# A graph layer with a fast convolution: tensor work moved off GpSimd, a first group that starts with its first weights, one pool of PSUM banks, and an instruction order from a model of three engines

## The chip, the cores and the metric

The kernel runs on one core of one Trainium2 chip, in fp32. The metric is the device time of one execution in microseconds (us). Each version was executed several times; nearly all times lie within 0.3% of their version's median. The engines are TensorE (PE in the profile; PEld is its weight load, which overlaps it), VectorE (DVE), ScalarE (ACT), GpSimd (POOL) and SyncE (SP, which issues most transfers). The profile shows one execution: for the kernel before a further one (2689 us, 0.6% under the median). So a span differs a little from the median.

## The reference

32 graphs of 512 nodes with 256 features go through a layer norm and a relu, then one graph layer, then a residual addition. Cut to what matters:

```python
h = jnp.maximum(_layernorm(x, axis=-1), 0.0)
# the graph layer, with x now meaning h and xc its transpose per graph
y  = relu(bn1(conv1d(xc, conv1_w, pad=0)))          # 1 tap, 256 -> 256
y  = bn2(conv1d(y, conv2_w, pad=8))                 # 17 taps, 256 -> 256
x_conv = relu(y + xc)
s = x @ w_se.T + b_se                               # 3 numbers for each node
dist = sq[:, :, None] + sq[:, None, :] - 2.0 * einsum('bnd,bmd->bnm', s, s)
A = exp(-dist) * mask                               # 512 x 512 for each graph
x_nmp = einsum('bnm,bmd->bnd', A, relu(x @ w_msg.T + b_msg))
gi, gh = concat([x_conv, x_nmp]) @ w_ih.T + b_ih, x @ w_hh.T + b_hh
r, z = sigmoid(gi_r + gh_r), sigmoid(gi_z + gh_z)
n = tanh(gi_n + r * gh_n)
out = x_before_the_norm + (1.0 - z) * n + z * x
```

## The kernel before

The 17-tap convolution is not done tap by tap. Four graphs form a group, there are 8 groups, and each group's convolution is a set of 25 small products (5 outer times 5 inner points of evaluation), so 200 products in all. A product needs a weight tile `w` of three 256x256 matrices (two taps and their sum) and an operand `x2` made from the first convolution's output. It multiplies the common column of `x2` by the sum `w[:, 2]` into PSUM tile `ps_b`, and the two differences `xd` by the two taps into `ps_c`: 12 matmuls where direct evaluation takes 16. VectorE adds the parts and puts the 25 products together again. Only then can a group's gates run, because they need all of its convolution.

The weights are made once on VectorE, ScalarE and GpSimd, written to DRAM, and read back for every group. No product may start before all 25 are made and a second lane of three graphs is through:

```python
    def ends(x2):
        xd = cv.tile([P, 2, RV], F32, name="xd", bufs=2)
        ...
        nc.gpsimd.tensor_tensor(
            xd, d02, x2[:, 1:2, :].to_broadcast([P, 2, RV]), op=ALU.subtract
        )
        return xd
    ...
            # in weights_first, for each of the 25 points
                w = cv.tile([P, 3, ND, D], F32, name="w", bufs=2)
                for i in range(ND):
                    nc.scalar.activation(
                        w[:, :2, i, :], next(inner[i]), AF.Copy, scale=GSCALE[j1] * GSCALE[j2]
                    )
                    yield
                nc.gpsimd.tensor_tensor(w[:, 2], w[:, 0], w[:, 1], op=ALU.add)
                if made is not None:
                    nc.scalar.dma_start(WD[made_w], made)
                    made_w += 1
    ...
    def convolution():
        wg = (w for _ in range(NG) for w in weights_again())
        yield lambda: made_w == 25 and not lanes[1].batches
        ...
                while len(WS) < min(m + 1 + AHEAD_W, 25 * NG):     # AHEAD_W is 1
                    WS.append(next(wg))
```

PSUM has eight banks here: two for `ps_c`, one for `ps_b`, two for the gates' `ps_acc`, two for `ps_g`, and one, `ps_tr`, that nearly all transposes by TensorE share:

```python
    gps = ctx.enter_context(tc.tile_pool(name="gps", bufs=2, space=PSUM))
    tr = ctx.enter_context(tc.tile_pool(name="tr", bufs=1, space=PSUM))
```

GpSimd also does the last three steps of the gates, and VectorE does the scaling of the layer norm:

```python
                nc.gpsimd.tensor_tensor(t, hT[:, o, :], r, op=ALU.subtract)
                nc.gpsimd.tensor_tensor(t, z, t, op=ALU.mult)
                nc.gpsimd.tensor_tensor(t, r, t, op=ALU.add)
```

The order of the instructions on each engine is fixed when the program is built. Streams of work (normalisation, graphs, convolution, gates, output) are Python generators; each reports how much PE time it has used, and a function `pace` hands out VectorE and ScalarE work in proportion to it, whether or not those engines are then free.

## Time and profile before

| | before |
|---|---|
| median of 3 runs (a fourth came with the comparison) | 2703.95 us (2698.34 to 2708.66) |
| span in the profile | 2687.0 us |
| PE work if every matmul ran back to back at full clock ("warm"; the prediction derives it) | 2074 us |
| end of product 25 (first group) | 419 us |
| mean granted PE clock | 0.925 |
| GpSimd tensor work that the change moves | 605 us |

The last row is the sum of the busy times of five kinds of GpSimd instruction: 283.2 (`xd`), 98.5, 94.8 and 93.1 (the gates' mixes) and 35.3 (the third weight matrix).

The way to read this kernel is as a ledger of PE. The span is PE's warm work plus what is lost, and what is lost is either idle PE or PE that is busy below its full clock. I keep this ledger for two stages, the start (until product 25 ends) and the rest. The ends of products are read from the records that write `ps_c`; the warm work that the program issues up to product 25 is counted from the instructions in their order. The prediction shows the lines.

### The profile page before, as it was taken

To read this page: it belongs to the slowest core of one execution; us is meant where nothing else is said; L and a number is where in the kernel's file an instruction comes from. 1 tells how busy PE (TensorE), PEld (TensorE's weight loads), DVE (VectorE), ACT (ScalarE), POOL (GpSimd) and SP (SyncE) were. 2 spreads that over 40 slices of the span, in tenths; PEclk is the share of its full clock that TensorE was granted. 3 is DMA by queue.
4 is the path that set the end of the run, shared out by engine and by line. 5 is a ranking of instruction groups with operands and counts; after the bars stand their busy time and mean duration, and the time that the engine had idled before them with its cause. 6 is when DMAs were issued, how large, how long until landed. Compare 5 with 4: busy or idle time off the path is not lost. (4 is left out here: it accounts for less than half of the span.)

```text
span 2687.0 us, 25967 instructions
## 1 busy us (share of the span) xinstructions
PE 2267.2 (84%) x9312; PEld 1385.3 (52%) x9312; DVE 1471.7 (55%) x2461; ACT 712.1 (27%) x1184; POOL 642.0 (24%) x468
## 2 busy tenths in 40 slices
PE   5537786888878899989899888998998899899998
PEld 2214665455445555555555555565555555555443
DVE  5663786455447556455646546575645555656311
ACT  3232223322324222332232421333231312211211
POOL 1130221121112212222212222222213222333222
PEclk8767898988989999989999999999999999999999
DMA  6464655344335434343444334554433333423211
GB/s 198 140 222 123 207 185 168 83 130 145 113 110 143 125 121 129 141 153 110 134 128 125 117 123 149 153 157 118 126 118 135 119 118 129 145 94 124 85 60 35
DMA packets 388240, 351.84 MB, mean 131 GB/s; under 512 B 280720, under 2 KB 330256, under 8 KB 387472
## 3 DMA queue, kind: packets, MB, share of 16 engines
q1 hardware_dynamic: 370688, 296.96, 36.9%
q10 hardware_dynamic: 17424, 53.22, 5.1%
q8 instruction: 74, 1.21, 0.2%
q14 instruction: 54, 0.44, 0.1%
HBM read 280.12 MB, written 69.99 MB: 130 GB/s over the span
## 5 line engine op out<-in xcount | busy, mean ns | idle before, releaser
L98 PEld LDWEIGHTS ps_c<-xd,w 128*128 128x128 f32 x3200 | 412.5, 205 | 88.7 <-issue 46.5
L98 PE MATMUL ps_c<-xd,w 128*128 128x116 f32 x3200 | 422.4, 289 | 35.8 <-POOL xd L345 35.8
L345 POOL TENSOR_TENSOR xd<-x 128x480 f32<-128x480 f32 x200 | 283.2, 1423 | 686.7 <-PE ps_c L98 296.2
L744 PE MATMUL ps_acc<-xconv,wih 128*128 128x512 f32 x768 | 372.8, 609 | 6.4 <-ACT xconv L755 6.4
L744 PE MATMUL ps_acc<-hTb,whh 128*128 128x512 f32 x768 | 371.7, 616 | 3.7 <-ACT r L763 3.7
L98 PE MATMUL ps_b<-x,w 128*128 128x116 f32 x1600 | 238.6, 297 | 152.0 <-DMA w<-wd 97.5
L744 PE MATMUL ps_acc<-xnb,wih 128*128 128x512 f32 x768 | 363.6, 596 | 0.0
L781 POOL TENSOR_TENSOR o_sb<-hTb,r 128x512 f32<-128x512 f32 x64 | 93.1, 1454 | 1014.8 <-ACT r L776 1014.8
L98 PEld LDWEIGHTS ps_b<-x,w 128*128 128x128 f32 x1600 | 223.6, 210 | 215.2 <-issue 151.9
L775 DVE TENSOR_TENSOR r<-ps_acc,r 128x512 f32<-128x512 f32 x64 | 44.2, 691 | 383.2 <-PE ps_acc L744 383.2
L646 PE MATMUL ps_g<-at,msg 128*128 128x512 f32 x464 | 220.7, 624 | 17.7 <-DVE at L640 17.5
L744 PEld LDWEIGHTS ps_acc<-hTb,whh 128*128 128x128 f32 x768 | 145.3, 198 | 158.7 <-issue 150.2
L744 PEld LDWEIGHTS ps_acc<-xconv,wih 128*128 128x128 f32 x768 | 142.5, 195 | 153.3 <-issue 141.5
L744 PEld LDWEIGHTS ps_acc<-xnb,wih 128*128 128x128 f32 x768 | 141.4, 191 | 153.8 <-issue 153.3
L567 ACT ACTIVATE mid<-ps_b 128x232 f32<-128x232 f32 x200 | 72.7, 363 | 423.4 <-PE ps_b L98 396.7
L304 DVE SCALAR_TENSOR_TENSOR x<-x,x 128x480 f32<-128x480 f32 (+1 forms) x184 | 169.4, 920 | 2.3
L766 DVE SCALAR_TENSOR_TENSOR r<-ps_acc,vec,r 128x512 f32<-128x512 f32 x64 | 48.0, 749 | 218.1 <-PE ps_acc L744 180.7
L646 PEld LDWEIGHTS ps_g<-at,msg 128*128 128x128 f32 x464 | 91.3, 202 | 132.5 <-issue 113.8
L592 DVE TENSOR_TENSOR msg<-ps_g,bmsg 128x256 f32<-128x256 f32 x116 | 48.8, 421 | 175.8 <-PE ps_g L98 175.7
L98 PE MATMUL ps_g<-wmsg,hT 128*128 128x259 f32 x464 | 124.3, 410 | 16.7 <-DVE aug L593 10.8
L295 DVE TENSOR_TENSOR x<-x 128x240 f32<-128x240 f32 (+1 forms) x200 | 132.5, 662 | 0.9
L443 DVE TENSOR_TENSOR n<-ps_c,mid 128x464 f32<-128x464 f32 x120 | 76.0, 633 | 88.6 <-PE ps_c L98 87.4
(119 smaller groups left out, 2690.4 us busy)
## 6 DMA issues: line engine op xcount, KB each, us to landing
w<-wd SPq DMA_DIRECT2D x200, 768.0 KB, 4.6
m_sb<-in_adj_dram SPq DMA_DIRECT2D x512, 64.0 KB, 2.5
wd<-w ACTq DMA_DIRECT2D x25, 768.0 KB, 3.5
hd<-hT ACTq DMA_DIRECT2D x32, 512.0 KB, 6.5
nd<-right ACTq DMA_DIRECT2D x64, 256.0 KB, 2.0
hTb<-hd SPq DMA_DIRECT2D x32, 512.0 KB, 5.1
xnb<-nd SPq DMA_DIRECT2D x64, 256.0 KB, 2.9
res<-in_x_dram SPq DMA_DIRECT2D x64, 256.0 KB, 5.0
```

Of the source, the lines that this page charges most:

```text
L98: nc.tensor.matmul(ps, lhsT, rhs, start=(i == 0), stop=(i == len(pairs) - 1))
L295: nc.vector.tensor_tensor(dst[:, :some, :], get(a, some), get(b, some), op=ALU.subtract)
L304: nc.vector.scalar_tensor_tensor(dst, a, -2.0, b, op0=ALU.mult, op1=ALU.add)
L345: nc.gpsimd.tensor_tensor(xd, d02, x2[:, 1:2, :].to_broadcast([P, 2, RV]), op=ALU.subtract)
L443: nc.vector.tensor_tensor(dst.rearrange("p (h n) -> p h n", h=2), ps.rearrange("p (h n) -> p h n", h=2), mid[:, None, :].to_broadcast([P, ...
L567: nc.scalar.activation(mid, ps, AF.Copy)
L592: nc.vector.tensor_tensor(msg[:, c, :], ps[:, :D], bmsg[:, :D], op=ALU.add)
L646: nc.tensor.matmul(ps, msg[:, c, d * P : (d + 1) * P], at[:, c, :], start=(c == 0), stop=(c == NT - 1))
L744: nc.tensor.matmul(ps, w[:, at + i, cols(o, g)], hT[:, i, :] if k == 0 else x_in[2 * k - 2 + i], start=(k == of[0] and i == 0), stop=(k == ...
L766: nc.vector.scalar_tensor_tensor(r, ps_h, vec[:, _COL["b_hh"] + 2 * ND + o : _COL["b_hh"] + 2 * ND + o + 1], r, op0=ALU.add, op1=ALU.mult,)
L775: nc.vector.tensor_tensor(r, ps_n, r, op=ALU.add)
L781: nc.gpsimd.tensor_tensor(t, hT[:, o, :], r, op=ALU.subtract)
```

## The change

The intent: use GpSimd for nothing but tiny square roots and a few transfers, so that it cannot hold up VectorE; let the first group begin as soon as its first weight exists; give transposes the same banks as other work; and let a model of the engines choose the order. The core of the diff, with cuts and with comments added here:

```diff
-    gps = ctx.enter_context(tc.tile_pool(name="gps", bufs=2, space=PSUM))
-    tr = ctx.enter_context(tc.tile_pool(name="tr", bufs=1, space=PSUM))
+    gps = ctx.enter_context(tc.tile_pool(name="gps", bufs=3, space=PSUM))
+    now = 10.0
+    class Engine:
+        def __getattr__(self, name):
+            def issue(*tiles, **more):
+                size = max(elements(t) for t in tiles if hasattr(t, "shape"))
+                self.free = max(self.free, now) + self.fixed + self.each * size
+                getattr(self.engine, name)(*tiles, **more)
+            return issue
+    dve, act = Engine(nc.vector, 0.12, 0.00108), Engine(nc.scalar, 0.16, 0.0009)
+    def matmul(ps, lhsT, rhs, **more):
+        nonlocal now
+        now += max(0.22, elements(ps) / 600.0)
+        nc.tensor.matmul(ps, lhsT, rhs, **more)
...
-        nc.gpsimd.tensor_tensor(                   # xd; the gates' three mixes alike
+        dve.tensor_tensor(
             xd, d02, x2[:, 1:2, :].to_broadcast([P, 2, RV]), op=ALU.subtract
         )
...
-            nc.vector.tensor_scalar(               # scaling of the layer norm
-                xs[:, c, :], xs[:, c, :], mv[:, c, 0:1], rstd[:, c : c + 1],
-                op0=ALU.subtract, op1=ALU.mult,
+            act.activation(
+                xs[:, c, :], xs[:, c, :], AF.Identity, bias=shift[:, c : c + 1],
+                scale=rstd[:, c : c + 1],
             )
...
-        yield lambda: made_w == 25 and not lanes[1].batches
+                yield lambda: len(X2) > m and len(WS) > m
+                yield max(X_AT[m], W_AT[m])
+                if g == 0:                         # no xd, no third weight
+                    d0, d1, d2 = sides(x2[:, 0, :]), sides(x2[:, 1, :]), sides(x2[:, 0, :], 1)
+                    product(ps[:, :NH], (0, d0), (1, d1))
+                    product(ps[:, NH:], (0, d1), (1, d2))
...
-    AHEAD, AHEAD_W = 3, 1                          # two weight buffers, one product ahead
+        return cv.tile([P, 3, ND, D], F32, name="w", bufs=3)
+                while 25 <= len(WS) < min(m + 3, 25 * NG):
+                    weights_again(len(WS))
...
+        if b < TURNED:                             # the first 8 graphs' masks: turned by PE
+            m, ps = gr.masks.pop((b, c)), bank()
+            for k in range(NT):
+                turn(ps[:, k * P : (k + 1) * P], m[:, k * P : (k + 1) * P])
...
-        credit = min(credit + pe * rate, 1.0)      # pace()
+        while dve.free < now + 0.5 and background():   # fill()
+            pass
```

The second lane of graphs goes too. Third weights are made on VectorE during the second group and sent to DRAM from there on.

## The prediction

> **What bounds the kernel now.** I read the page's busy shares and slices first, then the busy times of two stretches, then what TensorE (PE) waited for in the second of them, and last the durations of VectorE (DVE) instructions beside GpSimd (POOL) ones.
>
> ```profile
> PE 2267.2 (84%) x9312; PEld 1385.3 (52%) x9312; DVE 1471.7 (55%) x2461; ACT 712.1 (27%) x1184; POOL 642.0 (24%) x468
> ...
> PE   5537786888878899989899888998998899899998
> ...
> PEclk8767898988989999989999999999999999999999
> ```
>
> PE is the busy engine, and no other is over 55%. But slices 1 to 5 (some 67 us each) are poor in PE work, and in the same slices the granted clock is down to 0.6 to 0.8. So there are two stages: a start, and a long rest.
>
> How much PE time is needed? The chain of waits shows dense runs at full clock (start us, us, what):
>
> ```profile
> 2137.45 1.79 PE ps_c L98 x16
> ...
> 2546.00 25.77 PE ps_acc L744 x60
> ```
>
> An fp32 matmul is two records here, so a convolution matmul of 116 columns costs 2 x 0.111 us and a matmul of 512 columns 2 x 0.429 us. From the records' starts in dense runs, one of 259 columns costs 2 x 0.218 and a 128x128 transpose 0.109; the eight records of one exponential's four products take about 1.2 us together. Over the whole program: 4800 x 0.111 + (2304 + 512 + 256) x 0.429 + 512 x 0.218 + 672 x 0.109 + 32 x 1.2 = 2074 us. This "warm floor" is 77% of the 2687 us span; 613 us are lost to idleness and to the low clock.
>
> The first convolution product starts at 258 us, and the first group's 25th ends at 419 us (from the starts of the records that write ps_c). By then 204 us of warm work are done. The two stretches (columns: busy of PE, PE weight load, DVE, ACT, POOL, then the clock):
>
> ```profile
> 0.00:419.00 419.00, 263.18 (x1121) 173.28 (x1122) 257.67 (x524) 118.95 (x233) 87.59 (x80) 0.81 0.58 179
> 419.00:2687.00 2268.00, 2004.07 (x8193) 1212.03 (x8192) 1214.08 (x1937) 593.16 (x952) 554.39 (x388) 0.95 0.39 122
> ```
>
> Start: 419 - 204 = 215 us lost. Rest: 2074 - 204 = 1870 us of warm work in 2268, so 398 us lost: 264 us of idle PE (2268 - 2004) and 134 us in which PE was busy but slower than warm. What the idle PE of the rest waited for (us in total, times, longest):
>
> ```profile
> PE ps_b L98 <- DMA w<-wd: 75.5, 26, 7.9
> PE ps_c L98 <- POOL xd L345: 35.6, 17, 6.7
> PE ps_tr L659 <- DVE res L663: 31.6, 32, 3.4
> PE ps_tr L616 <- ACT left L613: 22.3, 23, 2.8
> PE ps_b L98 <- ACT at L634: 20.4, 8, 6.6
> PE ps_tr L260 <- ACT hT L261: 16.4, 15, 2.0
> ```
>
> These are not one bottleneck but many short waits: a weight tile with one product's warning, the POOL difference, and transposes that share one PSUM bank (ps_tr, 31.6 + 22.3 + 16.4 = 70 us).
>
> Last, what POOL does to DVE. First two groups of DVE instructions (min/median/max ns):
>
> ```profile
> L304 DVE SCALAR_TENSOR_TENSOR x<-x,x x184: 624/657/2699, 91.0 to 2480.5; 128x480 f32<-128x480 f32 x160, 128x1440 f32<-128x1440 f32 x24
> ...
> L775 DVE TENSOR_TENSOR r<-ps_acc,r x64: 681/692/693, 516.1 to 2674.8; 128x512 f32<-128x512 f32 x64
> ```
>
> Then one moment of the timelines of DVE and POOL (start us, us):
>
> ```profile
> 1362.13 1.72 DVE L295 TENSOR_TENSOR x<-x 128x480 f32<-128x480 f32 x1
> ...
> 1361.79 1.54 POOL L783 TENSOR_TENSOR o_sb<-r,o_sb 128x512 f32<-128x512 f32 x1
> ```
>
> L295 takes 0.65 us when POOL is quiet; here it sits out L783 and takes 1.72. L775, with one input in PSUM, never varies. Taking every DVE form at its median beside no POOL work instead of its mean, DVE's summed durations fall from 1596 to 1417 us: POOL costs DVE 178 us.
>
> **What the Trainium skill says.** "SBUF — State Buffer", Who interferes with whom: DVE and GpSimd share a port pair under an exclusive lock; a DVE instruction with two SBUF inputs contends with GpSimd instructions that read SBUF, one with at most one SBUF input outside the two-port modes does not. The trace agrees, by L304 against L775 and by the single-input SBUF scaling L239 (406 ns, up to 1355). "GPSIMD Engine Reference", 4.1 Engine selection: two-input elementwise work is about twice as slow there as on DVE. Agrees: xd, 480 elements, is 1.20 us at the median on POOL, and DVE's undisturbed two-input form of that size 0.65. "TensorE: Matmul & The Clock Gate", HAM oscillation: idle gaps put the PE clock back to half. Agrees: the clock records hold only 0.5 and 1.0, and the poor slices are the cold ones.
>
> **The change, part by part.**
>
> *Work on PE.* The first group's products use both taps directly: 16 matmuls for 12, so 25 x 4 x 0.222 = +22 us. Eight graphs' masks are transposed on PE: 128 x 0.109 = +14. New floor 2110 us.
>
> *Start.* Before, 25 products waited for all 25 weights, written to DRAM and read back, and for three graphs of a second lane. Now each product goes once its own weight exists. In the new PE order the four first conv1 pairs (in the old kernel done at 72 us, with 12 us of waiting behind exponentials and a batch's transposes) come before any exponential, and the raw weights (issued at 31 us behind 19 mask loads) are asked for ahead of the masks. I choose 48 us for the first product: the fourth normalisation ended at 30 us before, and transposes, conv1 and six us of first operands follow. The new order shows 204 us of warm PE work up to product 25, of which some 17 lie before the first product. DVE must in the same time make weights (10 of 1.75 us and 50 of 0.69 = 52), operands of a group (47), the group's sums (34), six graphs (6 x 6) and six normalisations' statistics (15): 184 us. Neither engine has slack over the other, so I choose 85% of PE's warm rate: 48 + 187 / 0.85 = 268, say 270 us for product 25, against 419. That is the largest term, about -150.
>
> *DVE.* Gains 175 xd x 0.65 = 114, 192 gate mixes x 0.68 = 131, 25 third weights x 0.69 = 17, 32 small shifts 5: +267. Loses 128 scalings x 0.405 = 52 (to ACT), 32 mask transposes x 0.72 = 23, 25 first-group sums x 0.63 = 16 (to ACT): -91. Loses the lock: -178. Net -2: everything POOL did fits into the time POOL cost DVE. Over a shorter span DVE rises to about 61%.
>
> *ACT.* 128 scalings x 0.56 (the like-sized h with scale and bias) = +72, the first group's copies +14, its mids -9; its order has 52 table switches for 46 at 1.28 us, +8. About 800 us, no bound.
>
> *Rest.* Warm work 2110 - 204 = 1906. Idle: weights now come two products ahead in three buffers (I take 60 of 75), xd is ready on DVE a product ahead (30 of 36), transposes rotate through three banks with everything else (55 of 76, the 70 plus 5.5 us of L659 waiting on POOL): -145. Cold time shrinks in proportion, 134 x 145 / 264 = -74. Against this I set +45 of new waits, because DVE is in order and now holds xd and the mixes too. Lost: 398 - 145 - 74 + 45 = 224. Rest: 1906 + 224 = 2130.
>
> Sum: 270 + 2130 = 2400 us.
>
> **The rivals.** (1) *The new order brings as many waits as it removes.* It is fixed at build time from estimated durations; where they are off, an in-order engine holds everything behind it. A row load is no longer asked for one batch ahead, and four rows stand between two groups' operands. For it: PE idle is already spread over many small causes. Against: the named ones are structural and really go. The rest then keeps its 1870 / 2268 = 0.825: 1906 / 0.825 + 270 = 2580. (2) *DVE becomes the bound.* For it: more two-input work, and the start needs 184 us of it. Against: 61% on average. If the start runs at DVE's pace with gaps, product 25 falls at 320 and the rest loses 40 more: 2490. (3) *The order works as meant*, and PE runs the rest at 0.93, as the old kernel's last gates do (31.9 warm us in each 34.3 us round): 1906 / 0.93 + 260 = 2310. (4) *The start is hidden anyway.* Against it: no gate can run before the first group ends, so its 150 us cannot be won back elsewhere. A slower kernel would need 290 us of new waits over my sum; I see no source of that size.
>
> **Range and chances.** Rival 3 sets the low end, 2310; rival 2 with 20 us to spare sets the high end, 2510, so that rival 1 in full lies outside. The 2% line is 2650, above even rival 1: faster 0.95, same 0.04, slower 0.01.
>
> **What would show it.** First product near 48 us and product 25 near 270; POOL busy under 60 us; L304's maximum near its median for its form; DVE busy within 60 us of 1472; PE's waits for w and for the transposes' bank mostly gone; mean clock 0.97 or more. Wrong if product 25 comes after 320, if the rest runs under 0.85 of warm, or if PE waits long for DVE's xd or mixes.

## The result, and the profile after

| | before | after |
|---|---|---|
| median | 2702.93 us (4 runs) | 2331.05 us (4 runs, 2323.61 to 2335.55) |
| span in the profile | 2687.0 us | 2331.6 us |
| first product starts | 258 us | 54 us |
| product 25 ends | 419 us | 287 us |
| DVE: excess over undisturbed durations | 178 us | 1 us |

The ratio of the two is 0.8621 (95% interval 0.8591 to 0.865). Ratios are computed as the mean time of one kernel's runs over that of the other's of the same rounds, so they are not quite the ratio of the medians quoted.

The page of the kernel after: busy shares, PE and its clock in 40 slices, and the chain of work that ended last by engine:

```profile
PE 2186.6 (94%) x9640; PEld 1359.6 (58%) x9640; DVE 1453.7 (62%) x2700; ACT 783.0 (34%) x1318; POOL 60.6 (3%) x73
...
PE   5888989999989999999989998999999999999998
...
PEclk9998989999999999999999999999999999999999
...
PE 83%; DVE 6%; ACT 5%; DMA 4%; issue 1%; SPq 0%; ACTq 0%; DVEq 0%
```

One poor slice is left at the start, where five were; the clock is 0.975 on average; and 83% of the chain is PE's own work. GpSimd is down to 60.6 us. The kernel is now bound by PE in the plain sense.

The busy times of the two stretches, start and rest, in the columns that the prediction names:

```profile
0.00:287.00 287.00, 232.49 (x1291) 171.77 (x1291) 174.89 (x382) 125.87 (x243) 16.52 (x27) 0.93 0.44 159
287.00:2331.60 2044.60, 1954.10 (x8352) 1187.86 (x8350) 1278.77 (x2319) 657.10 (x1075) 44.09 (x46) 0.98 0.47 145
```

The program again issues 204 us of warm work up to product 25. So the start loses 287 - 204 = 83 us, where it lost 215. The rest has 2110 - 204 = 1906 us of warm work in 2044.6, so it loses 138.6 us: 2044.6 - 1954.1 = 90.5 idle, and 1954.1 - 1906 = 48.1 below full clock. Before, it lost 398 (264 and 134).

What PE waited for in the rest (us in total, times, longest):

```profile
PE ps_acc L126 <- ACT r L117: 13.3, 11, 5.1
PE ps_g L126 <- DVE aug L117: 13.2, 4, 9.3
PE ps_c L126 <- DVE xd L117: 12.2, 5, 6.5
PE ps_c L126 <- DVE z L117: 8.9, 3, 4.5
PE ps_g L126 <- DVE res L117: 8.6, 2, 5.9
PE ps_b L126 <- ACT at L117: 7.0, 6, 2.7
...
PE ps_g L131 <- DVE o_sb L117: 4.2, 2, 3.6
```

L126 and L131 are the helpers through which nearly all matmuls and transposes pass, L117 the one for VectorE and ScalarE work, so one goes by the tiles and not by the lines. The 75.5 us for `w` are gone from the list, and the transposes that waited for their bank from its top. No cause is left that is worth 1% of the span.

The durations of single VectorE instructions (min/median/max ns), which answer the question of the lock (GpSimd holding up VectorE):

```profile
L117 DVE SCALAR_TENSOR_TENSOR x<-x,x x184: 624/651/1659, 50.4 to 2145.6; 128x480 f32<-128x480 f32 x160, 128x1440 f32<-128x1440 f32 x24
...
L117 DVE TENSOR_TENSOR xd<-x x175: 625/650/660, 285.5 to 2146.3; 128x480 f32<-128x480 f32 x175
```

The maximum of 1659 ns is that of the 24 long instructions of 1440 elements; among those of 480 elements nothing now stands out. Before, the same group went up to 2699 ns.

Last, the timeline of PE around the first product:

```profile
42.01 3.70 PE L126 MATMUL ps_g<-hT,w 128*128 128x512 f32 x8 [0.30 <-ACT hT L117]
...
53.27 1.11 PE L131 MATMUL ps_g<-ident,x_sb 128*128 128x128 f32 x4 [5.13 <-ACT left L117]
54.17 8.84 PE L126 MATMUL ps_c<-x,w 128*128 128x116 f32 x64
```

The last pair of the first convolution starts at 42 us and the first product at 54 us, 6 us later than I chose.

### The profile page after: what moved, and what is told of

Read it like the earlier page. It is cut to its first block, busy times and chain, and to the rows that moved or that the text cites. A ratio compares the mean times of both kernels' runs of the same rounds, so it can differ in the third digit from the quotient of the medians.

```text
span 2331.6 us, 26175 instructions
## 1 busy us (share of the span) xinstructions
PE 2186.6 (94%) x9640; PEld 1359.6 (58%) x9640; DVE 1453.7 (62%) x2700; ACT 783.0 (34%) x1318; POOL 60.6 (3%) x73
## 4 chain that ended last, share of the span: by engine, by line
PE 83%; DVE 6%; ACT 5%; DMA 4%; issue 1%; SPq 0%; ACTq 0%; DVEq 0%
PE ps_acc L126 40%; PE ps_g L126 17%; PE ps_c L126 16%; PE ps_b L126 6%; PE ps_g L131 3%; DMA nd<-right 1%; PE ps_b L724 1%; DMA res<-in_x_dram 1%; DVE o_sb L117 1%; ACT at L117 1%; ACT r L117 1%; DMA w<-wd 1%; DMA xnb<-nd 1%; DVE x L117 1%; ACT L117 1%
## 5 line engine op out<-in xcount | busy, mean ns | idle before, releaser
L126 PE MATMUL ps_acc<-hTb,whh 128*128 128x512 f32 x768 | 366.3, 607 | 13.3 <-ACT r L117 13.3
L126 PE MATMUL ps_c<-xd,w 128*128 128x116 f32 x2800 | 349.6, 279 | 21.1 <-DVE xd L117 12.2
L126 PE MATMUL ps_acc<-xconv,wih 128*128 128x512 f32 x768 | 363.9, 596 | 4.6 <-ACT xconv L117 4.6
L126 PE MATMUL ps_acc<-xnb,wih 128*128 128x512 f32 x768 | 362.7, 594 | 2.8 <-DMA xnb<-nd 2.6
L126 PEld LDWEIGHTS ps_c<-xd,w 128*128 128x128 f32 x2800 | 334.2, 195 | 25.3 <-DVE xd L117 13.1
L126 PE MATMUL ps_g<-at,msg 128*128 128x512 f32 x512 | 233.5, 604 | 11.8 <-DVE at L117 10.2
L126 PEld LDWEIGHTS ps_acc<-hTb,whh 128*128 128x128 f32 x768 | 142.9, 194 | 169.8 <-issue 141.9
L126 PEld LDWEIGHTS ps_acc<-xnb,wih 128*128 128x128 f32 x768 | 141.5, 189 | 165.1 <-issue 158.2
L126 PEld LDWEIGHTS ps_acc<-xconv,wih 128*128 128x128 f32 x768 | 141.8, 191 | 160.3 <-issue 149.7
L126 PEld LDWEIGHTS ps_b<-x,w 128*128 128x128 f32 x1400 | 182.8, 193 | 77.1 <-issue 58.0
L117 DVE TENSOR_TENSOR r<-ps_acc,r 128x512 f32<-128x512 f32 x64 | 44.2, 691 | 267.0 <-PE ps_acc L126 267.0
L126 PE MATMUL ps_b<-x,w 128*128 128x116 f32 x1400 | 185.6, 276 | 7.2 <-ACT at L117 7.0
L117 ACT ACTIVATE mid<-ps_b 128x232 f32<-128x232 f32 x175 | 63.6, 363 | 339.2 <-PE ps_b L126 322.3
L126 PEld LDWEIGHTS ps_g<-at,msg 128*128 128x128 f32 x512 | 96.9, 194 | 126.5 <-issue 109.5
L117 DVE SCALAR_TENSOR_TENSOR r<-ps_acc,vec,r 128x512 f32<-128x512 f32 x64 | 48.0, 751 | 184.1 <-PE ps_acc L126 149.5
L126 PE MATMUL ps_g<-wmsg,hTg 128*128 128x259 f32 x512 | 131.9, 395 | 23.2 <-DVE aug L117 13.2
L117 DVE SCALAR_TENSOR_TENSOR x<-x,x 128x480 f32<-128x480 f32 (+1 forms) x184 | 143.8, 782 | 2.0
L117 ACT ACTIVATE right<-ps_g 128x512 f32<-128x512 f32 x96 | 57.3, 597 | 257.7 <-PE ps_g L126 227.5
L117 ACT ACTIVATE z<-ps_acc,brz 128x512 f32<-128x512 f32 x64 | 43.9, 686 | 276.0 <-PE ps_acc L126 275.9
L117 DVE TENSOR_TENSOR x<-x 128x240 f32<-128x240 f32 (+1 forms) x320 | 135.6, 462 | 0.3
L126 PEld LDWEIGHTS ps_g<-wmsg,hTg 128*128 128x128 f32 x512 | 97.3, 196 | 61.6 <-issue 35.3
L126 PE MATMUL ps_g<-hT,w 128*128 128x512 f32 x256 | 123.9, 630 | 3.9 <-ACT hT L117 2.7
```

The lines of the kernel that those rows point to most:

```text
L117: getattr(self.engine, name)(*tiles, **more)
L126: nc.tensor.matmul(ps, lhsT, rhs, **more)
```

## The experiments

Twelve kernels were run. Most go back from the kernel after by one part; two put one part into the kernel before. Each ran four times, beside seven runs of the kernel before on the same chip, whose medians were 2696 to 2700 us against 2703 in the first comparison; so I read no difference under 10 us. The kernel after was not run again in these rounds: a loss against it compares medians of different rounds, and comes out up to 8 us larger if the ratios to the kernel before are compared instead. This is the ledger of all of them from their traces (us). The warm work up to product 25 is 204, but 194 for e4, 225 for e8, 240 for e6 and 197 for e7 and e11, because the order differs.

| run | median | ratio to before | warm work | lost, start | lost, rest |
|---|---|---|---|---|---|
| before | 2703 | 1 | 2074 | 215 | 398 |
| after | 2331 | 0.862 | 2110 | 83 | 139 |
| e1_both_pool | 2360 | 0.875 | 2110 | 84 | 164 |
| e2_before_dve | 2700 | 1.001 | 2074 | 227 | 402 |
| e3_w_one_ahead | 2372 | 0.879 | 2110 | 83 | 178 |
| e4_all_weights_first | 2331 | 0.865 | 2110 | 87 | 130 |
| e5_one_transpose_bank | 2467 | 0.914 | 2110 | 108 | 244 |
| e6_model_2p5 | 2814 | 1.043 | 2110 | 121 | 590 |
| e7_model_pe_1p5 | 2401 | 0.890 | 2110 | 100 | 188 |
| e8_first_group_12 | 2370 | 0.878 | 2088 | 142 | 140 |
| e9_before_shared_banks | 2593 | 0.960 | 2074 | 200 | 318 |
| e10_four_undone | 2516 | 0.933 | 2110 | 112 | 290 |
| e11_masks_on_vector | 2304 | 0.855 | 2096 | 100 | 103 |
| e12_model_evacuation | 2336 | 0.866 | 2110 | 77 | 143 |

### e1_both_pool: the moved work back on GpSimd, in the new order

```diff
+    class Booked(Engine):                      # issues on GpSimd, but is booked in the model as VectorE
+        ...
+                dve.free = max(dve.free, now) + dve.fixed + dve.each * size
+    pool = Booked(nc.gpsimd, 0.0, 0.0)
-        dve.tensor_tensor(                         # xd, and the three mixes alike
+        pool.tensor_tensor(
```

> The kernel after, with xd (175) and the gate mixes (192) issued on GpSimd again, their time still booked on VectorE in the model, so that the order on every engine stays as it is but for the moved instructions. Theory A (the lock and GpSimd's latency were on the path): VectorE's summed durations exceed their undisturbed medians by 130 to 180 us again, PE waits 30 us or more for xd, and the time is 2400 to 2460 us. Rival B (VectorE had slack, the gain is from order, buffers and start): the excess comes back all the same, but the time stays under 2365 us.

Measured: 2359.63 us, ratio 0.8748 (0.8728 to 0.8768), so some 29 us more than the kernel after, within rival B's range. The traces show the same order of TensorE's work, and of what is left on VectorE, in both kernels. VectorE's and GpSimd's durations in this run:

```profile
L117 DVE SCALAR_TENSOR_TENSOR x<-x,x x184: 625/652/2226, 50.8 to 2167.0; 128x480 f32<-128x480 f32 x160, 128x1440 f32<-128x1440 f32 x24
...
L126 POOL TENSOR_TENSOR xd<-x x175: 1186/1207/2645, 287.3 to 2169.9; 128x480 f32<-128x480 f32 x175
```

The long maxima are back on both engines, and so is VectorE's excess: the sum of its durations is 1510 us against 1347 undisturbed, 163 us. Of these 163 us only 26 appear in PE's ledger (84 + 164 against 83 + 139). So the excess comes with GpSimd's work, and the price of the move back is small. It is not the price of the lock alone: with the moved work VectorE also loses 245 us of its own (1592 undisturbed to 1347). VectorE is busy for 59% of this span; I take it that most of the excess falls into the other 41%, which no run shows.

### e2_before_dve: the same work taken off GpSimd in the kernel before

```diff
-        nc.gpsimd.tensor_tensor(                   # xd; third weight; three mixes
+        nc.vector.tensor_tensor(
```

> The kernel before, with xd (200), mixes (192) and third weights (25) on VectorE and nothing else changed. Theory A: the lock's excess of 178 us goes to nearly 0, the waits of PE for xd shrink, and the time falls to 2570 to 2640 us. Rival B: less than 40 us are gained (2665 or more), since the old order and the other waits hold it; rival C: VectorE in order delays PSUM evacuations and it gets slower.

Measured: 2700.21 us, ratio 1.001 (0.9988 to 1.0032): nothing. The VectorE group that the prediction shows, in this run:

```profile
L304 DVE SCALAR_TENSOR_TENSOR x<-x,x x184: 626/652/1660, 91.7 to 2482.1; 128x480 f32<-128x480 f32 x160, 128x1440 f32<-128x1440 f32 x24
```

The excess went from 178 us to 0.4. But VectorE took over some 281 us of work (undisturbed, 1417 to 1699), so it is busy for 1555 us here and was for 1472. The run prices the move, the freedom from GpSimd and the added work together, and not the lock alone. PE's waits over the whole span:

```profile
PE ps_b L98 <- DMA w<-wd: 117.2, 41, 11.8
PE ps_tr L260 <- ACT hT L261: 56.3, 24, 14.6
PE ps_tr L616 <- ACT left L613: 53.7, 32, 13.8
PE ps_tr L659 <- DVE res L663: 33.6, 32, 3.6
```

The old causes still lead, `w` with more than the 97.5 us it had over the whole span before. The wait for `xd` fell from 35.8 to 16.8 us, and that did not reach the end. So the part that names the change first, tensor work off GpSimd, is worth nothing in the old order and some 29 us in the new one.

### e3_w_one_ahead: two weight buffers, one product ahead

```diff
-        return cv.tile([P, 3, ND, D], F32, name="w", bufs=3)
+        return cv.tile([P, 3, ND, D], F32, name="w", bufs=2)
-                while 25 <= len(WS) < min(m + 3, 25 * NG):
+                while 25 <= len(WS) < min(m + 2, 25 * NG):
```

The weights of the first group are made one product ahead too (a third edit, left out here).

> The kernel after, with two weight buffers instead of three, asked for one product ahead instead of two. Theory A (the wait for w, 75 us before, went because of the third buffer): PE waits 50 us or more for w again and the time is 2385 to 2430 us. Rival (the new order spaces products so that one ahead suffices): under 20 us of such waits and at most 2350 us.

Measured: 2371.83 us, ratio 0.879 (0.8773 to 0.8808), some 41 us more, between the two expectations. PE's waits that are laid to `w` over the whole span:

```profile
PE ps_b L126 <- DMA w<-wd: 10.5, 6, 3.7
```

So the 39 us that the rest loses more are not all in this line; `w` holds 3% of the chain that ended last. I take it that a late weight also shifts the VectorE and ScalarE work behind that product; this run does not separate that.

### e4_all_weights_first: all 25 weights made and stored before the first product

```diff
+        yield lambda: made_w == 25
-                while 25 <= len(WS) < min(m + 3, 25 * NG):
+                while len(WS) < min(m + 3, 25 * NG):
```

Weights now go only to DRAM when made, and the first group reads them back, as in the kernel before.

> The kernel after, but the first group's products wait for all 25 weights, which are then read back from DRAM; both taps direct as in after. Theory A (weights as they are made are most of the start's gain): first product at 130 to 180 us instead of 54, product 25 at 340 us or later instead of 287, time 2385 to 2415 us. Rival (the start was won by the order, the early raw weights and the dropped second lane): product 25 before 310, time under 2355 us.

Measured: 2331.45 us, ratio 0.8651 (0.8627 to 0.8675): no loss. The timeline where the products begin:

```profile
141.74 29.34 PE L126 MATMUL ps_c<-x,w 128*128 128x116 f32 x256
```

and the two stretches up to and after 150 us:

```profile
0.00:150.00 150.00, 99.64 (x369) 59.42 (x370) 91.19 (x213) 78.47 (x151) 10.27 (x22) 0.84 0.67 243
150.00:287.00 137.00, 127.73 (x903) 108.30 (x903) 81.80 (x162) 47.08 (x90) 6.72 (x5) 0.99 0.51 174
```

The first product waits until 142 us, then PE runs products back to back at a clock of 0.99, and product 25 ends at 281 us, 6 us before that of the kernel after. VectorE's busy time up to 287 us is 91.2 + 81.8 = 173 us here and 174.9 there: the same work has to be done before product 25 in both. Whether the products go in between or at the end made no difference to when that work and the 25th product were done. This refutes, in this order, the reason that I had given for the start, as far as it names the weights. The edit does not put back the other thing that the old kernel waited for, the second lane of graphs.

### e5_one_transpose_bank: the transposes in one bank again

```diff
-    gps = ctx.enter_context(tc.tile_pool(name="gps", bufs=3, space=PSUM))
+    gps = ctx.enter_context(tc.tile_pool(name="gps", bufs=2, space=PSUM))
+    tr = ctx.enter_context(tc.tile_pool(name="tr", bufs=1, space=PSUM))
-        ps = bank()          # where the output is transposes, and in one of four exponential products
+        ps = turn_bank()
```

> The kernel after, with all transposes (rows, factors, masks, results) in one PSUM bank of their own, as before, and two banks instead of three for the rest. Theory A (the shared three banks removed the some 76 us that PE waited for the one bank): PE waits 40 us or more for that bank and the time is 2380 to 2430 us. Rival (the new order spaces the transposes, the bank is no bound): under 20 us of such waits and at most 2350 us.

Measured: 2467.12 us, ratio 0.9137 (0.9121 to 0.9153), 136 us more, above both expectations. PE's waits over the whole span:

```profile
PE ps_tr L132 <- DVE res L118: 63.5, 33, 7.3
PE ps_tr L132 <- ACT hT L118: 32.4, 31, 2.9
PE ps_tr L132 <- ACT left L118: 31.8, 31, 7.5
```

The transposes of the outputs wait 33 times for the residual addition of the pair before, 1.9 us each (32 times and 1.0 us in the kernel before), and the other two kinds come back with it: 127.7 us in three lines. The turned masks pass through this bank too, which the kernel before did not have; they waited 8.8 us for VectorE's reading of it. The ledger puts 25 us of the loss into the start and 106 into the rest.

### e6_model_2p5 and e7_model_pe_1p5: the same instructions in a worse order

In e6 the model believes that VectorE and ScalarE are 2.5 times as slow, in e7 that TensorE is 1.5 times as slow. The instructions are those of the kernel after; only their order changes, and with it how often ScalarE loads a table (14 times in e6 and 54 in e7, for 52).

```diff
-    dve, act = Engine(nc.vector, 0.12, 0.00108), Engine(nc.scalar, 0.16, 0.0009)
+    dve, act = Engine(nc.vector, 0.3, 0.0027), Engine(nc.scalar, 0.4, 0.00225)     # e6
...
-        now += max(0.22, elements(ps) / 600.0)
+        now += max(0.33, elements(ps) / 400.0)                                     # e7
```

> The kernel after with nothing changed but the model: VectorE and ScalarE taken 2.5 times as slow as they are when the order is made. Same instructions, another order. Theory A (the order from right durations is the main gain of the long rest): 2430 us or more, with PE idle 180 us or more. Rival (any order with enough buffers does as well): 2360 us or less.

> The kernel after with the model's matmul 1.5 times as slow as it is, so that VectorE and ScalarE look quicker beside PE than they are. Theory A: 2400 us or more, with PE waiting for VectorE and ScalarE results. Rival: 2360 us or less.

Measured: e6 2813.83 us, ratio 1.0426 (1.0402 to 1.045), slower than the kernel before although every structural gain is in it; e7 2400.85 us, 0.8899 (0.8882 to 0.8916). PE's waits over the span of e6:

```profile
PE ps_g L126 <- DMA hTg<-hd: 123.6, 19, 11.3
PE ps_g L126 <- DVE at L117: 76.5, 48, 6.9
PE ps_acc L126 <- ACT xconv L117: 44.9, 16, 12.3
```

A graph's input is asked for too late, and PE stands 19 times for up to 11 us; masked exponentials and convolution results are issued too late on their own engines. None of these leads the list of the kernel after. So my first rival, an order that brings as many waits as the structure removes, is a real danger: it costs 483 us here. The constants as they stand avoid it. No run lies between these scalings and the model as it stands, so there is no curve of time against model error.

### e8_first_group_12: the first group with 12 matmuls for each product

```diff
-                if g == 0:
+                if g < 0:                          # xd for every product
+                yield act.free + 0.1
+                dve.tensor_tensor(w[:, 2], w[:, 0], w[:, 1], op=ALU.add)
```

> The kernel after, but the first group's products as in the other groups: third weight and differences xd on VectorE, 12 matmuls instead of 16. 22 us less of warm PE work, some 49 us more of VectorE work before product 25. Theory A (the start is bound by VectorE as much as PE): product 25 at 300 us or later and 2335 to 2365 us. Rival (the start is bound by PE): product 25 at 270 us or earlier and 2305 to 2325 us.

Measured: 2369.64 us, ratio 0.8776 (0.8763 to 0.8789), 39 us more although PE has 22 us less to do, and just above theory A's range. The stretch up to product 25:

```profile
0.00:367.00 367.00, 280.35 (x1267) 194.60 (x1267) 234.13 (x510) 138.24 (x275) 16.57 (x26) 0.86 0.42 141
```

Product 25 ends at 367 us. VectorE is busy for 234 us in it, 59 us more than in the start of the kernel after. Some 47 us of these are the work that e8 adds (third weights 16, `xd` 16, sums 15); the rest belongs to graphs that fall into the longer stretch. The start loses 142 us, 59 more than 83; that both figures are 59 is chance. So PE loses at least what VectorE got to do, although VectorE is busy for only 175 of the 287 us of the start in the kernel after. Whether it is VectorE's load, or that each weight and operand now passes VectorE once more before its product, this run does not separate. Using both taps directly spends 22 us of PE work to spare VectorE the third weights and the differences, and wins. Part of the 80 us comes back, because 21 us more PE work was already done by product 25.

### e9_before_shared_banks: one pool of banks in the kernel before

```diff
-    gps = ctx.enter_context(tc.tile_pool(name="gps", bufs=2, space=PSUM))
-    tr = ctx.enter_context(tc.tile_pool(name="tr", bufs=1, space=PSUM))
+    gps = ctx.enter_context(tc.tile_pool(name="gps", bufs=3, space=PSUM))
-        ps = tr.tile([P, N], F32, name="ps_tr")    # four places
+        ps = gps.tile([P, N], F32, name="ps_g")
```

> The kernel before, with its one transpose bank and its two other banks made one pool of three, as in after; order, GpSimd work and weight buffers as before. Theory A (the bank is worth its waits in any order): PE's waits for transposes fall by 50 us or more and the time is 2640 us or less. Rival (like the lock, it is worth little in the old order, since another wait takes its place): 2670 us or more.

Measured: 2593.06 us, ratio 0.9599 (0.9558 to 0.9641): 104 us from a few lines (95 in the traces, 15 of them in the start). PE's waits over the span, and then the stretch of the rest:

```profile
PE ps_b L97 <- DMA w<-wd: 111.5, 35, 9.9
PE ps_c L97 <- POOL xd L344: 35.4, 16, 6.7
PE ps_b L97 <- ACT at L633: 20.6, 9, 4.6
```

```profile
404.00:2592.00 2188.00, 1983.53 (x8188) 1216.18 (x8187) 1214.51 (x1937) 589.73 (x951) 555.14 (x388) 0.95 0.41 127
```

The transposes' waits, 31 to 63 us each over the whole span before, are gone from the top; `w` and `xd` stay. The idle PE of the rest falls from 264 to 2188 - 1984 = 204 us, by 60, and the time below full clock from 134 to 1984 - 1870 = 114, by 20. It is the larger by far of the two parts that were tried in the old order.

### e10_four_undone: e1, e3, e4 and e5 together

```diff
+    tr = ctx.enter_context(tc.tile_pool(name="tr", bufs=1, space=PSUM))    # e5
+    pool = Booked(nc.gpsimd, 0.0, 0.0)                                      # e1
-        return cv.tile([P, 3, ND, D], F32, name="w", bufs=3)
+        return cv.tile([P, 3, ND, D], F32, name="w", bufs=2)                # e3
+        yield lambda: made_w == 25                                          # e4
```

> The kernel after with four parts undone together: xd and mixes on GpSimd, two weight buffers, one transpose bank, all weights first. Undone one at a time they cost about 28, 40, 136 and 0 us. If they add up: 2535 us. If they are the same waits seen twice: 2460 to 2500 us. If they compound: 2580 us or more. What then still lies below 2700 us is the order's, with scaling on ScalarE, masks on PE and direct taps.

Measured: 2516.19 us, ratio 0.9333 (0.9303 to 0.9362), 185 us above the kernel after. The single losses are 29, 41, 0 and 136 us, together 206, so they nearly add. With all four gone the kernel is still 181 us below the kernel before of the same rounds. In the traces it is 2687 - 2512 = 175: 103 us less lost in the start and 108 in the rest, against 36 us more PE work. These 211 us, a little over half of the 391 us by which the change cut the losses, belong to what was not undone: the order, the scaling on ScalarE, the direct taps (59 of the start's, if e8's figure carries over), the masks, the third weights on VectorE, and the one lane of graphs. No run divides them further.

### e11_masks_on_vector: no masks turned by TensorE

```diff
-TURNED = 8
+TURNED = 0
```

> The kernel after with no mask transposed on PE: 14 us less of warm PE work, 22 us more of VectorE work in the first eight graphs, and the mask loads of these in small pieces again. Theory A (the start is bound by VectorE and loads): product 25 at 300 us or later and 2335 to 2365 us. Rival (bound by PE): product 25 by 280 us and 2315 to 2330 us.

Measured: 2303.97 us (2300.51 to 2310.93), ratio 0.855 (0.8516 to 0.8585). This beats both kernels; e12 in the same rounds, which is the kernel after but for one constant of the model, took 2336.30. Both expectations missed: product 25 ends at 297 us, 10 later, and the time is below both ranges.

```profile
PE 2165.2 (94%) x9512; PEld 1350.1 (59%) x9512; DVE 1475.4 (64%) x2732; ACT 784.0 (34%) x1318; POOL 61.8 (3%) x73
```

PE has 128 transposes, 14 us of warm work, less, and VectorE is busy for 22 us more. With the turned masks the start loses 17 us less, but the rest loses 36 us more, and only the first two groups' graphs are concerned. The order is made anew by the model when this constant changes; product 100 ends at 1069 us against 1071, product 200 at 2132 against 2154. So most of the gain comes late, long after the last mask that TensorE turns (the last starts at 545 us in the kernel after). I cannot say more than that this order happens to be better; no run turns all masks on TensorE, and none holds the late order fixed.

### e12_model_evacuation: a truer duration for one ScalarE instruction

```diff
+        act.free += 0.6                            # after each evacuation y -> xconv
```

The model gives this instruction 0.63 us (0.16 + 522 x 0.0009), and the trace of the kernel after shows 1.33 us.

> The kernel after with the model told what the trace shows of one term it has wrong: an evacuation of the convolution's sums takes ScalarE 1.25 us, the model books 0.63; 0.6 us are added. Theory A (a truer model gives a better order): 2300 to 2322 us. Rival (the order is good enough, other errors weigh more): 2323 to 2345 us.

Measured: 2336.30 us, ratio 0.8661 (0.8634 to 0.8689): no gain. One constant that is off by half is not what keeps PE idle.

## Why the prediction was right or wrong

The direction and the time are right (2400 predicted with 2310 to 2510, measured 2331), and the named marks of the profile came nearly all: POOL 60.6 us for "under 60" (just over), DVE 1453.7 us for 1472 within 60, ACT 783 for about 800, L304's successor without outliers, the clock 0.975. Several steps of the working were nevertheless wrong or wrongly sized, and that the sum came as near as it did is in part luck.

**Start: the size nearly right, the named cause wrong as far as it was tested.** The sum had 270 us for product 25; it was 287: the first product came 6 us later, and PE then ran at (204 - 17) / (287 - 54) = 0.80 of its warm rate for 0.85. But the sentence "Before, 25 products waited for all 25 weights, written to DRAM and read back" as the reason for the gain fails by e4: with that wait put back, product 25 ends at 281 us. The early first product (54 us) alone is worth nothing. The sentence goes on "and for three graphs of a second lane", and this half no run puts back. It is a rival: in the trace of the kernel before the last weight is sent off at 202 us, while PE is at the last work of that lane (`ps_acc<-at,msg`) from 256.6 us and starts the first product at 258.4. e8 points to VectorE's part before each product as what decides when product 25 can end, which is nearer to rival 2 than to the waiting that I named. What the runs show in its place: the direct taps (59 us less lost, e8), the shared banks (25 us, e5; 15 us in the old kernel, e9), and 103 us that stay when GpSimd, banks, weights' wait and buffers are all undone (e10), which would include those 59. The weights also come later in the old kernel: the last one at 202 us, in e4 at 138 us. I have not separated whether the new order or the lighter VectorE does that.

**Lock: right, and rightly given little time.** I read from the trace that GpSimd cost VectorE 178 us, and the sum gave the move a net of -2 us on VectorE. The excess went to 1 us, came back to 163 in e1, and vanished in e2, and VectorE's summed durations went from 1596 to 1593 us. In time the move is worth 0 in the old order and 29 in the new one, and those 29 hold the slower `xd` and mixes as well. One reading of the prediction does not carry: L775 "never varies", but in the trace none of its 64 executions overlaps GpSimd's tensor work, so it shows nothing of the lock. Another line of the kernel before does. L443, also with one input in PSUM, overlapped it in 90 of 200 executions, and its longest took 643 ns:

```profile
L443 DVE TENSOR_TENSOR n<-ps_c,mid x120: 621/631/643, 261.3 to 2504.1; 128x464 f32<-128x464 f32 x120
```

For `xd` in the rest I had put 30 us, 45 with its share of cold time (134 x 30 / 264 = 15); e1's rest lost 25 more.

**Banks: right to a few us for the rest of the old kernel.** "55 of 76" with its share of cold time (134 x 55 / 264 = 28) is 83; e9 shows 60 + 20 = 80 in the rest. What I did not count is the start's part. In the new, denser order one bank costs more, 106 us in the rest (e5), there with the turned masks in it as well.

**Weights: too large.** "60 of 75", with its cold time (134 x 60 / 264 = 30) 90, against 39 in e3's rest. In the new order the rest loses 25 us by e1, 39 by e3 and 106 by e5, together 170, and 290 - 139 = 151 with all of them in one kernel (e10), where my sum had 145 + 74 = 219. So the counted parts brought less than I said, with more on the banks and less on the weights.

**The step that failed: "+45 of new waits, because DVE is in order and now holds xd and the mixes too".** Here lies the reason why the rest took 2045 us where I had 2130. Lost in the rest: 224 predicted, 139 measured. Idle PE was 90 where I had 264 - 145 + 45 = 164, and the time below full clock 48 where I had 134 - 74 = 60. The new waits did not come: for `xd` and the mixes PE waited 12.2 + 4.2 us in the rest of the kernel after, and 35.6 + 5.5 us before (`xd` and `o_sb` on GpSimd), and with both back on GpSimd the rest loses 25 us more (e1). Besides, the sum had no term for what the rest of the change takes away there: with the four counted parts undone the rest still loses 108 us less than before (e10). So the working reads 398 - 219 + 45 = 224 as predicted and 398 - 151 - 108 = 139 as measured: what stood as +45 beside the counted parts is -108, 153 us away, and the counted parts, too large by 68, make up for some of it. The 108 us hold the order, the scaling on ScalarE and the single lane, so how much of it is the order alone stays open. The other rivals: rival 1's mechanism is real, but only for a bad model (e6); rival 3, PE at 0.93 in the rest, is what happened (1906 / 2044.6 = 0.93), together with a start that is 27 us longer than the rival had.

**PE's added work.** The +22 us for direct taps buy more than they cost (e8). The +14 us for turned masks do not, as the whole program with its order stands (e11).

## What to carry to other kernels

Contention that shows in an engine's durations is not yet time lost: here the move that ended it gained nothing in the old order. Try such a part alone in the old kernel before counting on it. A small dedicated buffer, here one PSUM bank for all transposes, was worth 104 us by a few lines in the old kernel and 136 in the new one. When a program is in order on every engine, its order can be worth as much as all the rest of the design: the same instructions took from 2331 to 2814 us.

## What the Trainium skill lacked or had wrong

- "SBUF — State Buffer", Who interferes with whom: the rule held (643 ns at most for L443, with one input in PSUM; up to 2699 for L304, with two in SBUF). It lacks that the lock's cost on the durations says little of the time: moving the work, with 178 us less contention and 281 us more work on VectorE, changed the time by a factor of 1.001 (e2), and moving it back, with 163 us more contention and 245 us less work, cost 29 us (e1).
- "Perfetto Trace Analysis", Matmuls and Matmul Optimizations: it advises that independent matmul groups rotate through different banks, so that the reading of one overlaps the next, and that all eight banks be used. The runs agree with the first. But both kernels use all eight; what mattered is whether the transposes share the rotation with other work: 104 us in one order (e9), 136 us in the other (e5). The page gives no number for this.
- "ScalarE: Activation LUTs", What ACT_TABLE_LOAD costs: an estimate by its formula is 186 + 2 x 93 + 0.833 x 522 = 807 ns for an activation of 522 elements with two pointer operands, and the one from `y` to `xconv`, which rearranges its elements, took 1329 ns on average; for the plain one of 256 elements (`x_sb`) the estimate is 585 ns, and 595 ns were measured. The section gives no cost for strides; that they are the cause here was not tested.
- No page has how much the order of instructions on in-order engines is worth: 2331 to 2814 us for the same instructions (after, e6), and 32 us between two kernels of the same rounds that differ in who turns eight graphs' masks and in the order that follows from it (e11, e12).
